# Layer 0's softmax sums in four 32-column tiles, with the reciprocals spread by DMA

## The chip, the core and the metric

The kernel runs on one core of a Trainium2 chip. The metric is the time of one execution in microseconds (us). PE is the matmul engine (TensorE), ACT is ScalarE, DVE is VectorE, POOL is GpSimd; SP is the engine that issues most DMAs. [...] the runs shown agree within 0.1%.

## What is computed

Two layers follow each other on four images of 32x32 tokens with 768 channels. Each adds to its input an attention of 12 heads of 64 channels, with a bias by row and by column of the image. The change touches the end of layer 0's attention:

```python
attn = (attn.reshape(b * NH, h, w, h, w) + rel_bias_h[:, :, :, :, None] + rel_bias_w[:, :, :, None, :]).reshape(b * NH, hw, hw)
attn = jax.nn.softmax(attn, axis=-1)
out = jnp.einsum('bqk,bkd->bqd', attn, v)
```

The kernel takes exponentials of the scores without their maximum, multiplies them by the values, and divides by the sum of the exponentials afterwards. So for every query of every head it needs one sum over 1024 keys and one reciprocal of it, and 64 channels of the result are multiplied by that reciprocal.

## The kernel before

The work is ordered in stages: (image 0, layer 0), (image 1, layer 0), (image 0, layer 1), (image 1, layer 1), and then the same for images 2 and 3. A stage has six pairs of heads; a pair fills the 128 partitions, one head in each half. `attend` (L720) handles one pair. It takes the queries in two halves c of QC = 512 columns, and the keys of each in two groups of four tiles of 128. For a group PE computes the scores s (L820) and adds the bias (L822), ACT takes the exponentials e (L827), and after some other work PE multiplies them by the values into av (L844). In layer 0 DVE adds the eight exponential tiles of a half into `acc` (L836, L838), one column block for each head.

The order on PE, ACT, DVE and POOL is the order in which the program is written; only SP's queue is ordered by the framework. `attend` gives way four times in each half, and a table of events runs pieces of other work at these steps: the next pair's projections and its bias (`positions`, PE line L613, tile rel), the projection of the stage before, weights that are mixed in the first stage, normalisation.

What is left to do for a half when its av is finished is held in the list `rest` and done one part at a time by `more()`, which is called four times in a half: after the scores and after the products with the values of each key group. For layer 0 the parts are `sums`, `result` and `finish`:

- `copy` (L742), at once: ACT copies av from PSUM into `weighed`, which has one buffer.
- `sums` (L788 to L793), at the first call of the next half: PE multiplies a matrix of ones with `acc` into the PSUM tile z, for each head 64 columns of ones, so that all 64 partitions of the head hold the same sums (two matmuls of 512 columns; L789). ACT copies z to t, and takes Ln and Exp of it to get a first reciprocal `inv`.
- `result` (L800, L801, L807), at the second call: DVE corrects the reciprocal by one Newton step in two instructions, and multiplies `weighed` by it.
- `finish` (L812), at the third: ACT adds the bias of the values and writes the result over the pair's q.

Layer 1 gets its sums in another way, from a column of ones among the values; its first DMAs (L748, L749) carry one row of `weighed` to DRAM and spread it over 64 partitions into t, issued by POOL. It shares `weighed`, t and inv with layer 0. `put_q`, `put_k` and `centre`, `back` (PE lines L556, L591; tiles ln_c, ln_t) make layer 1's queries and keys; DVE's taps (L542, L544) are its convolutions. The last pair of a layer-0 stage that is followed by layer 1 has these beside its own attention.

Weight loads for the projections go through SP (L250, L253, L254, L263) into two buffers: the load for the use after the next is issued when a use is done.

Of the kernel before, what the change touches and what calls it, by code (L numbers as in the profile page):

```python
# [9 lines left out]
F32 = mybir.dt.float32  # L10
F32R = mybir.dt.float32r
I32 = mybir.dt.int32
AF = mybir.ActivationFunctionType
ALU = mybir.AluOpType
# [3 lines left out]
P = 128  # L18
B = 4
S = 32  # L20
T = S * S
C = 768
NC = C // P
D = 64
HALF = T // 2
QC = 512
# [7 lines left out]
LN = 75  # L34
# [3 lines left out]
IDENT, GROUP, CENTRE, HEADS, ONES, WHOLE = 0, P, 2 * P, 3 * P, 3 * P + 2, 3 * P + 2 + D  # L38
# [7 lines left out]
def two_layers(ctx: ExitStack, tc: tile.TileContext, keep, x_in, wqkv, wproj, rels, windows, vrow, small, const, onehot, picks, out):  # L46
# [19 lines left out]
    nc = tc.nc  # L66
    pool = lambda name, bufs, **kw: ctx.enter_context(tc.tile_pool(name=name, bufs=bufs, **kw))
    fixed = pool("fixed", 1)
    dram = pool("dram", 1, space=bass.MemoryType.DRAM)
    xnp = pool("xnp", 1)  # L70
    wp = pool("wp", 2)
    work = pool("work", 2)
    one = pool("one", 1)
# [41 lines left out]
    def other_work(places):  # L115
        turn[:] = places
        place_b.n = place_c.n = 0
# [7 lines left out]
    def small_bank(name):  # L125
        return ps_small.tile([P, 512], F32, tag="small", name=name)
# [14 lines left out]
    cst = fixed.tile([P, NCONST], F32, tag="cst", name="cst")  # L141
# [5 lines left out]
    def col(c, lo=0, hi=P):  # L147
        return sm[lo:hi, c : c + 1]
# [222 lines left out]
    seen = fixed.tile([P, 2 * len(items) * (T // QC)], F32, tag="seen", name="seen")  # L371
    tiny = fixed.tile([P, 1], F32, tag="tiny", name="tiny")
# [342 lines left out]
            return pieces  # L715


    rest, found = [], ()

    def attend(pair, os):  # L720


        q, k, bias = pair.q, pair.k, pair.bias


        by_ones = [pair.layer and (pair.i < len(items) - 1 or c < T // QC - 1) for c in range(T // QC)]
        os.append(q)
        nonlocal found
        heads = [slice(j * D, (j + 1) * D) for j in range(2)]

        def more():
            nonlocal found
            if rest:
                found = rest.pop(0)(*found)

        for c in range(T // QC):
            cols = slice(c * QC, (c + 1) * QC)

            def copy(av, ones=by_ones[c]):

                weighed = one.tile([P, QC], F32, tag="weighed", name="weighed")
                nc.scalar.copy(weighed, av)  # L742
                if not ones:
                    return weighed, acc
                t = work.tile([P, QC], F32, tag="t", name="t", bufs=1)

                z = dram.tile([2, QC], F32, tag="z", name="z", bufs=2)
                nc.gpsimd.dma_start(z, weighed[D - 1 :: D, :])  # L748
                nc.gpsimd.dma_start(t, z.unsqueeze(1).to_broadcast([2, D, QC]))  # L749
                return weighed, t  # L750

            def restore(weighed):

                ps = small_bank("whole")
                halves(ps, cst[:, WHOLE : WHOLE + P], weighed)
                nc.scalar.copy(weighed, ps)

            def restore_last(weighed):

                ps = small_bank("last")  # L760
                odd = cst[:, WHOLE + 1 : WHOLE + P : 2]
                for h in range(2):
                    nc.tensor.matmul(
                        ps[h * D : (h + 1) * D, : QC // 2], odd, weighed[:, h * (QC // 2) : (h + 1) * (QC // 2)],
                        start=True, stop=True,
                    )
                last = one.tile([P, QC // 2], F32, tag="last", name="last")
                nc.scalar.copy(last, ps[:, : QC // 2])  # L768
                for h in range(2):
                    rows = last[h * D + D // 2 - 1 : (h + 1) * D : D // 2, :]  # L770
                    nc.gpsimd.dma_start(weighed[D - 1 :: D, h * (QC // 2) : (h + 1) * (QC // 2)], rows)  # L771

            def landed(*found):

                return found

            def sums(weighed, of, c=c, ones=by_ones[c]):

                at = 2 * (pair.i * (T // QC) + c)
                inv = work.tile([P, QC], F32, tag="inv", name="inv", bufs=1)  # L780
                if ones:
                    t = of
                    restore_last(weighed)
                    nc.scalar.activation(inv, t, AF.Copy, accum_out=seen[:, at : at + 1])
                else:
                    z = small_bank("z")
                    t = work.tile([P, QC], F32, tag="t", name="t", bufs=1)
                    for j, rows in enumerate(heads):  # L788
                        nc.tensor.matmul(z[rows, :], cst[:, ONES : ONES + D], of[:, j, :], start=True, stop=True)  # L789
                    nc.scalar.activation(t, z, AF.Copy, accum_out=seen[:, at : at + 1])  # L790

                nc.scalar.activation(inv, t, AF.Ln, bias=tiny)
                nc.scalar.activation(inv, inv, AF.Exp, scale=-1.0, accum_out=seen[:, at + 1 : at + 2])  # L793
                if pair.layer and not ones:
                    restore(weighed)
                return weighed, t, inv

            def result(weighed, t, inv, cols=cols):

                nc.vector.scalar_tensor_tensor(t, t, -1.0, inv, ALU.mult, ALU.mult)  # L800
                nc.vector.scalar_tensor_tensor(inv, t, 2.0, inv, ALU.add, ALU.mult)  # L801

                if pair.layer:
                    nc.vector.tensor_tensor(inv, weighed, inv, ALU.mult)
                    nc.vector.scalar_tensor_tensor(q[:, cols], inv, col(LN + 4), q[:, cols], ALU.mult, ALU.add)
                else:
                    nc.vector.tensor_tensor(inv, weighed, inv, ALU.mult)  # L807
                return (inv,)

            def finish(inv, cols=cols):  # L810

                nc.scalar.activation(q[:, cols], inv, AF.Identity, bias=col(pair.column(2)))  # L812

            for g in range(0, NKT, 4):
                es = []
                for kt, place in zip(range(g, g + 4), (None, place_b, place_c, None)):
                    keys = slice(kt * P, (kt + 1) * P)
                    ps = place.pair("s") if place else ps_a.tile([P, 2, 512], F32, tag="a", name="s")
                    for j, rows in enumerate(heads):
                        nc.tensor.matmul(ps[:, j, :], k[rows, keys], q[rows, cols], start=True, stop=False)  # L820
                    for j, rows in enumerate(heads):
                        nc.tensor.matmul(  # L822
                            ps[:, j, :], ones[rows, kt % 2 * P : (kt % 2 + 1) * P], bias[c][rows, kt // 2, :],
                            start=False, stop=True,
                        )
                    e = work.tile([P, 2, QC], F32, tag="e", name="e", bufs=4)
                    nc.scalar.activation(e, ps, AF.Exp)  # L827
                    es.append(e)
                other_work(behind_scores)
                more()  # L830
                if g == 0:
                    av = ps_av.tile([P, QC], F32, tag="av", name="av")
                if not by_ones[c]:
                    if g == 0:
                        acc = work.tile([P, 2, QC], F32, tag="acc", name="acc", bufs=1)
                        nc.vector.tensor_tensor(acc, es[0], es[1], ALU.add)  # L836
                    for e in es[2 * (g == 0) :]:
                        nc.vector.tensor_tensor(acc, acc, e, ALU.add)  # L838
                yield
                yield  # L840
                for t, e in enumerate(es):
                    kt = g + t
                    for j in range(2):
                        nc.tensor.matmul(  # L844
                            av[j * D : (j + 1) * D, :], pair.vt[:, kt, j * D : (j + 1) * D], e[:, j, :],
                            start=(kt == 0), stop=(kt == NKT - 1),
                        )
                other_work(behind_av)
                more()
                if g + 4 == NKT:  # L850

                    n_parts = 2 if short(pair.i) and (pair.hp, c) in ((NC - 2, 1), (NC - 1, 0)) else 1
                    rest.extend((landed,) * n_parts + (sums, result) if pair.layer else (sums, result, finish))
                    found = copy(av)
                yield
                yield
# [161 lines left out]
    for k, stage in enumerate(stages):  # L1018
        call, sums, products = project(stage, oss[k])
# [27 lines left out]
    for _ in range(2):  # L1047
        found = rest.pop(0)(*found)
    next(products)
    for part in rest:  # L1050
        found = part(*found)
# [314 lines left out]
```

## Time and profile before

| | |
|---|---|
| median of 3 runs | 3814.33 us (3814.24 to 3817.77) |
| the profiled execution, whole | 3816.61 us |
| its span in the trace | 3814.6 us |
| granted PE clock | 0.997 of full |
| z, t (ACT copy), Ln, Exp: each | 4 matmul records, 0.60, 0.72, 0.63 us |
| DVE's two steps of the correction, each | 0.68, 0.69 us |
| DMA to landing: mid<-x (256 KB, SP) | 3.1 us |
| DMA to landing: t<-z (256 KB, POOL) | 8.0 us |
| DMA to landing: z<-weighed (4 KB, POOL) | 1.6 us |

In lines of groups the first columns are the line, engine, operation, output and inputs; for PE the tile shape follows (rows*columns of the array), then the operands' shape and the count; behind the first bar stand the total busy time in us and the mean of one in ns; behind the second the idle time of the engine just before. In the list of waits the numbers are the total in us, the times and the longest. In the timeline the first two numbers are the start and the busy time in us, and brackets at the end hold the idle time before and what ended it. [...] records overlap; the distance between starts is the time that the work takes.

### The profile page before, as it was taken

The numbers are of one execution on the slowest core, as the hardware profiler recorded it, in microseconds if no ns is written. First come the engines' busy times: TensorE is split into PE (matmuls) and PEld (weight loads), VectorE is DVE, ScalarE is ACT, GpSimd is POOL, SyncE is SP. The second block draws the span as 40 slices with busy tenths as digits, with TensorE's granted clock in tenths as the row PEclk, the third lists the DMA queues.
The fourth block names the chain that finished last, engine by engine and source line by source line (L and its number), as shares of the span: only waits on it lengthen the run. The fifth ranks groups of instructions, "written<-read, shape, count | busy, mean of one in ns | idle before, by whom it ended". The sixth has DMA issues, their size and how long they took to land. (4 is left out here: it accounts for less than half of the span.)

```text
span 3814.6 us, 76313 instructions
## 1 busy us (share of the span) xinstructions
PE 3749.5 (98%) x32990; PEld 1656.7 (43%) x32990; DVE 2467.1 (65%) x3068; ACT 1786.5 (47%) x2573; POOL 529.1 (14%) x964
## 2 busy tenths in 40 slices
PE   8999999999999999999999999999999999999998
PEld 4535535533344443444535445355343444434442
DVE  2566554559678877688454554445686888867874
ACT  2455434545355553455534544254442555525562
POOL 0111100111111211111200010001111112111120
PEclk9999999999999999999999999999999999999999
DMA  4344443331431223311333132523114212142123
GB/s 152 102 122 116 134 144 90 101 81 40 119 102 48 57 59 95 123 48 48 82 111 121 53 78 63 171 61 78 46 46 131 87 50 66 47 122 65 48 58 100
DMA packets 214024, 330.44 MB, mean 87 GB/s; under 512 B 50390, under 2 KB 103698, under 8 KB 213680
## 3 DMA queue, kind: packets, MB, share of 16 engines
q1 hardware_dynamic: 122912, 211.86, 17.9%
q0 software_dynamic: 90768, 113.61, 12.6%
q8 instruction: 263, 4.31, 0.5%
q14 instruction: 81, 0.66, 0.1%
HBM read 184.23 MB, written 40.10 MB: 59 GB/s over the span
## 5 line engine op out<-in xcount | busy, mean ns | idle before, releaser
L827 ACT ACTIVATE e<-s 128x1024 f32<-128x1024 f32 x768 | 775.6, 1024 | 423.7 <-PE s L822 393.6
L131 PE MATMUL qkv<-xn,wqkv_t 128*64 128x512 f32 x3648 | 816.0, 596 | 7.0 <-DVE gmean L334 2.6
L820 PE MATMUL s<-q,k 64*128 64x512 f32 x3072 | 808.7, 603 | 6.6 <-ACT e L827 3.1
L544 DVE SCALAR_TENSOR_TENSOR shared<-shared,sm 128x1056 f32<-128x1056 f32 x576 | 757.9, 1316 | 15.7
L822 PE MATMUL s<-bias,ones 64*128 64x512 f32 x1536 | 611.7, 790 | 1.1 <-DMA bias<-whole 1.0
L844 PE MATMUL av<-e,vt 128*64 128x512 f32 x2624 | 596.2, 596 | 0.0
L131 PEld LDWEIGHTS qkv<-xn,wqkv_t 128*64 128x64 f32 x3648 | 256.5, 137 | 484.0 <-issue 466.1
L640 POOL DMA_DIRECT2D bias<-high x384 | 205.6, 556 | 1794.6 <-ACT high L629 1559.7
L838 DVE TENSOR_TENSOR acc<-acc,e 128x1024 f32<-128x1024 f32 x294 | 360.0, 1225 | 114.0 <-ACT e L827 87.4
L820 PEld LDWEIGHTS s<-q,k 64*128 64x128 f32 x3072 | 279.5, 186 | 264.4 <-issue 213.3
L527 ACT ACTIVATE shared<-qkv,sm 128x512 f32<-128x512 f32 (+1 forms) x288 | 129.3, 502 | 469.7 <-PE qkv L131 469.7
L844 PEld LDWEIGHTS av<-e,vt 128*64 128x64 f32 x2624 | 185.4, 137 | 350.9 <-issue 316.8
L822 PEld LDWEIGHTS s<-bias,ones 64*128 64x128 f32 x1536 | 148.6, 187 | 185.4 <-issue 184.1
L640 POOL DMA_DIRECT2D bias<-whole x384 | 207.2, 571 | 53.2 <-DVE whole L630 46.3
L836 DVE TENSOR_TENSOR acc<-e 128x1024 f32<-128x1024 f32 x49 | 60.0, 1225 | 215.4 <-ACT e L827 206.8
L742 ACT COPY weighed<-av 128x512 f32<-128x512 f32 x96 | 56.3, 587 | 279.0 <-PE av L844 270.1
L559 DVE TENSOR_REDUCE mean<-ln_c 128x8 f32<-128x512 f32 x144 | 98.6, 685 | 106.0 <-PE ln_c L556 106.0
L771 POOL DMA_DIRECT2D weighed<-last x94 | 50.7, 541 | 679.6 <-ACT last L768 638.6
L613 PEld LDWEIGHTS rel<-q,rel 64*32 64x32 f32 x6144 | 112.1, 106 | 68.6 <-issue 63.8
L613 PE MATMUL rel<-q_t,rel 64*32 64x32 f32 x6144 | 123.6, 195 | 1.8 <-issue 1.8
L613 PE MATMUL rel<-q,rel 64*32 64x32 f32 x6144 | 122.7, 195 | 1.9 <-issue 1.9
L412 DVE TENSOR_TENSOR shared<-shared,m3m 128x512 f32<-128x512 f32 x66 | 45.3, 687 | 119.9 <-PE m3m L131 119.8
(162 smaller groups left out, 4439.0 us busy)
## 6 DMA issues: line engine op xcount, KB each, us to landing
bias<-high POOLq DMA_DIRECT2D x384, 128.0 KB, 2.9
bias<-whole POOLq DMA_DIRECT2D x384, 128.0 KB, 3.0
wqkv_t<-in_wqkv SPq DMA_DIRECT2D x78, 384.0 KB, 3.2
wqkv_t<-mixed SPq DMA_DIRECT2D x66, 384.0 KB, 3.1
wproj_t<-mixed SPq DMA_DIRECT2D x48, 384.0 KB, 3.3
wqkv_t<-in_wqkv SPq DMA_DIRECT2D x66, 192.0 KB, 2.5
xn<-in_x SPq DMA_DIRECT2D x24, 512.0 KB, 7.7
x<-in_x SPq DMA_DIRECT2D x48, 256.0 KB, 3.2
```

Of the source, the lines that this page charges most:

```text
L131: nc.tensor.matmul(ps[lo : lo + D], a[:, lo : lo + D], b, start=start, stop=stop, **kw)
L527: nc.scalar.activation(self.pad[s][:, rows, there : there + src.shape[2]], src, AF.Identity, bias=col(self.column(s)))
L544: nc.vector.scalar_tensor_tensor(y, window, tap, y, ALU.mult, ALU.add)
L559: nc.vector.tensor_reduce(of, heads, AX.X, ALU.add)
L613: nc.tensor.matmul(ps[lo : lo + S, k * S : (k + 1) * S].rearrange("p (b c) -> p b c", b=2), rel[rows, 2 * self.layer + i, first : first + ...
L640: nc.gpsimd.dma_start(sets, some.unsqueeze(1).to_broadcast([D // 2, 2, QC]))
L820: nc.tensor.matmul(ps[:, j, :], k[rows, keys], q[rows, cols], start=True, stop=False)
L822: nc.tensor.matmul(ps[:, j, :], ones[rows, kt % 2 * P : (kt % 2 + 1) * P], bias[c][rows, kt // 2, :], start=False, stop=True,)
L827: nc.scalar.activation(e, ps, AF.Exp)
L836: nc.vector.tensor_tensor(acc, es[0], es[1], ALU.add)
L838: nc.vector.tensor_tensor(acc, acc, e, ALU.add)
L844: nc.tensor.matmul(av[j * D : (j + 1) * D, :], pair.vt[:, kt, j * D : (j + 1) * D], e[:, j, :], start=(kt == 0), stop=(kt == NKT - 1),)
```

## The change

For all layer-0 halves but the last of each stage, `sums` multiplies `acc` by 32 columns of ones instead of 64, and takes each head's 512 columns in two parts of 256: four matmuls, each into its own 32 partitions of z. ACT's copy, Ln and Exp and DVE's correction then work on 256 columns. `spread` writes one row of each 32 (4 rows of 256) to DRAM from SP's queue; `call`, one step later, reads it back over 64 partitions for each head into t. `spread_finish` puts the multiplication into a list `unfinished`; the next call of `more()`, the first of the half after, takes it from there, and the one after that writes q. So the product comes two calls after its reciprocals are called, and q is written three calls later than before. The last half of a stage keeps the old way, and before it reuses t what is unfinished is done at once. `weighed` gets two buffers, in both layers.

```diff
         def more():
             nonlocal found
+            for piece in [unfinished.pop() for _ in range(len(unfinished))]:
+                piece()
+            if rest and getattr(rest[0], "reuses", False):
+                while unfinished:
+                    unfinished.pop()()
             if rest:
                 found = rest.pop(0)(*found)
...
-                weighed = one.tile([P, QC], F32, tag="weighed", name="weighed")
+                weighed = one.tile([P, QC], F32, tag="weighed", name="weighed", bufs=2)
...
+                if not pair.layer and not last(c):
+
+                    z = small_bank("z")
+                    for j in range(2):
+                        for h in range(2):
+                            g, n = 2 * j + h, QC // 2
+                            nc.tensor.matmul(
+                                z[g * S : (g + 1) * S, :n], cst[:, ONES : ONES + S], of[:, j, h * n : (h + 1) * n],
+                                start=True, stop=True,
+                            )
+                    both = work.tile([P, 2, QC // 2], F32, tag="inv", name="z_inv", bufs=1)
+                    t, inv = both[:, 0], both[:, 1]
+                    nc.scalar.activation(t, z[:, : QC // 2], AF.Copy, accum_out=seen[:, at : at + 1])
+                    nc.scalar.activation(inv, t, AF.Ln, bias=tiny)
+                    nc.scalar.activation(inv, inv, AF.Exp, scale=-1.0, accum_out=seen[:, at + 1 : at + 2])
+                    return weighed, t, inv
...
+            def last(c):
+
+                return (pair.hp, c) == (NC - 1, T // QC - 1)
+
+            sums.reuses = last(c)
...
+            def spread(weighed, t, inv):
+
+                newton(t, inv)
+                z = dram.tile([2, QC], F32, tag="z_inv", name="z_inv", bufs=2)
+                nc.sync.dma_start(z.rearrange("j (h x) -> (j h) x", h=2), inv[S - 1 :: S, :])
+                return weighed, z
+
+            def call(weighed, z):
+
+                t = work.tile([P, QC], F32, tag="t", name="t", bufs=1)
+                nc.sync.dma_start(t, z.unsqueeze(1).to_broadcast([2, D, QC]))
+                return weighed, t
+
+            def spread_finish(weighed, t, cols=cols):
+
+                def multiply():
+                    nc.vector.tensor_tensor(t, weighed, t, ALU.mult)
+                    unfinished.append(lambda: finish(t, cols))
+
+                unfinished.append(multiply)
+                return ()
...
-                    rest.extend((landed,) * n_parts + (sums, result) if pair.layer else (sums, result, finish))
+                    rest.extend((landed,) * n_parts + (sums, result) if pair.layer else (sums, result, finish) if last(c) else (sums, spread, call, spread_finish))
```

`newton` holds DVE's two instructions of L800 and L801.

More of the change, by code (lines that the diff above doesn't have):

```diff
@@ L715, in plan @@
             return pieces
-    rest, found = [], ()
+    rest, found, unfinished = [], (), []
     def attend(pair, os):
@@ L796, in sums, with newton, result @@
                 return weighed, t, inv
-            def result(weighed, t, inv, cols=cols):
+            def last(c):
+                return (pair.hp, c) == (NC - 1, T // QC - 1)
+            sums.reuses = last(c)
+            def newton(t, inv):
                 nc.vector.scalar_tensor_tensor(t, t, -1.0, inv, ALU.mult, ALU.mult)
                 nc.vector.scalar_tensor_tensor(inv, t, 2.0, inv, ALU.add, ALU.mult)
[L803 to L808, printed above, removed]
+            def result(weighed, t, inv, cols=cols):
+                newton(t, inv)
+                nc.vector.tensor_tensor(inv, weighed, inv, ALU.mult)
+                if not pair.layer:
+                    return (inv,)
+                nc.vector.scalar_tensor_tensor(q[:, cols], inv, col(LN + 4), q[:, cols], ALU.mult, ALU.add)
+                return ()
+            def spread(weighed, t, inv):
+                newton(t, inv)
+                z = dram.tile([2, QC], F32, tag="z_inv", name="z_inv", bufs=2)
[10 more added lines that the diff above has]
+                unfinished.append(multiply)
+                return ()
             def finish(inv, cols=cols):
                 nc.scalar.activation(q[:, cols], inv, AF.Identity, bias=col(pair.column(2)))
+                return ()
             for g in range(0, NKT, 4):
```

## The prediction

> **What bounds the kernel now.** I read the page's busy shares first, then the waits of the matmul engine, then the groups by line for the rows that the change touches, then the timeline around them.
>
> ```profile
> PE 3749.5 (98%) x32990; PEld 1656.7 (43%) x32990; DVE 2467.1 (65%) x3068; ACT 1786.5 (47%) x2573; POOL 529.1 (14%) x964
> ```
> ```profile
> PE p1p L131 <- DVE os_sums L923: 7.4, 8, 1.6
> PE ln_t L591 <- DVE shared L560: 6.1, 7, 1.9
> ...
> PE s L820 <- ACT e L827: 3.1, 3, 1.4
> ```
> ```profile
> L789 PE MATMUL z<-acc,cst 128*64 128x512 f32 x196 | 52.8, 617 | 0.0
> L807 DVE TENSOR_TENSOR inv<-weighed,inv 128x512 f32<-128x512 f32 x48 | 33.2, 692 | 1.6
> L812 ACT ACTIVATE q<-inv,sm 128x512 f32<-128x512 f32 x48 | 34.2, 712 | 0.0
> L763 PE MATMUL last<-weighed,cst 128*64 128x256 f32 x188 | 28.9, 381 | 0.0
> ```
>
> PE is busy 98% of the span, and the largest waits of single causes on it are a few us over the whole run. So only two things can move the time: fewer cycles that PE streams, and one of the few places where another engine holds it. VectorE and ScalarE have a third to a half of the span free; their savings count only at such places. The sums of exponentials (z) are 196 matmul records for 49 pieces of work, four each: two heads in two column halves, and each float32 product in two passes. They never wait (idle 0.0).
>
> Now the same block in the timeline, three times:
>
> ```profile
> 201.56 1.08 PE L789 MATMUL z<-acc,cst 128*64 128x512 f32 x4
> 202.47 2.74 PE L131 MATMUL m4m<-xn,wqkv_t 128*64 128x512 f32 x12
> ```
> ```profile
> 237.93 1.08 PE L789 MATMUL z<-acc,cst 128*64 128x512 f32 x4
> 238.94 0.21 PE L613 MATMUL rel<-q,rel 64*32 64x32 f32 x1
> ```
> ```profile
> 1050.03 0.60 PE L763 MATMUL last<-weighed,cst 128*64 128x256 f32 x4
> 1050.46 1.89 PE L131 MATMUL qkv<-xn,wqkv_t 128*64 128x512 f32 x8
> ```
>
> From start to start, z costs 0.91 us when the next work has the same tile shape (128*64), and 1.01 us when the shape changes behind it (rel, 64*32): the change of shape costs 0.10. The row "last" has half the columns (256) in the same two column halves and costs 0.43. So time follows the columns streamed, 0.21 us per pass of 256 columns, with two column halves side by side.
>
> [...] No row of before shows four 128-row tiles of 32 columns; the nearest is rel, whose four tiles (two row halves, four column groups) start every 7 to 10 ns (888.59, 888.59, 888.60, 888.61) and last 190 ns, so four column groups do run at once there, but each half of the rows feeds only two of them. [...] the trace's 4 KB z<-weighed lands in 1.6.
>
> **The change part by part.** Layer 0 has 48 pieces (24 pairs of heads, two halves of the queries); the last of each of its four stages keeps the old way, so 44 change.
>
> *Matmuls.* Per piece 2 matmuls of 64x512 become 4 of 32x256, all four at once if the tiles are independent: a pass falls from 0.43 to 0.21, two passes save 0.43 us. From this go: (a) the stagger of four starts instead of two, 14 ns per pass by the 7 ns between two starts, 0.03; (b) a change of shape behind z where there was none. By the order of instructions the 44 are followed by rel 21 times and ln_c twice (a change of shape before and after, so nothing new: the nearest price is again 0.10), and 21 times by 128*64 work (m4m 18, av 2, v 1). There I add 0.10 for the change and 0.05 for the first pass behind a change (by the starts of its single records z's own first pass, behind s, takes 0.48, the second 0.43). Sum: 23 x 0.40 + 21 x (0.40 - 0.15) = 9.2 + 5.3 = 14.5 us. Bounds: if the four share two streams, z stays 0.9 and the extra changes cost 21 x 0.15 + 44 x 0.03 = 4.5 us; if the shape changes cost nothing, 44 x 0.43 = 19.
>
> *ScalarE and VectorE arithmetic.* Copy, Ln and Exp go from 512 to 256 columns: about 0.21 us less each (the copies of this kernel take 0.586 at 512 and 0.372 at 256), 44 x 0.6 = 28 us of ScalarE. The two VectorE steps of the correction lose about 0.27 each (0.69 at 512 columns, 0.55 at 384, so some 0.41 at 256), 44 x 0.55 = 24 us. Both beside PE's work, worth nothing in general.
>
> *The place where they are worth something.* The last layer-0 pair of stages two and six prepares layer 1, and VectorE there is busy without a gap from 877 to 920 us (46.1 of 50 us from 880 to 930, and 46.4 from 2780 to 2830), and PE waits for it:
>
> ```profile
> 910.70 0.66 PE L591 MATMUL ln_t<-cst,shared 128*128 128x128 f32 x4
> 913.24 0.63 PE L591 MATMUL ln_t<-cst,shared 128*128 128x128 f32 x4 [1.88 <-DVE shared L560]
> ```
>
> In this stretch the correction is 0.55 shorter and its product (0.69) goes to the next pair, where VectorE has a gap of 2.4 us; the product of the piece before comes in at 876, in a gap of 0.7. That is 1.2 us earlier at 913, less some 0.2 to 0.4 of PE's gain from z there that VectorE doesn't pass on: 1 us a time, 2 us in all. Between 0 and 3.
>
> *Transfers on SP.* Each piece adds two issues to SP's queue: the reciprocals to DRAM (waits for VectorE's correction) and from there spread to 128 partitions (waits for the first to land and for the last reader of t). Behind them in the queue stand the weight loads. By the order of instructions the next old issue comes in nearly all pieces 6.6 us or more after the correction ended in the trace of before (186.3 behind 179.7), in two pieces 3.5; the pair takes some 0.4 to issue and 1.6 to 2 to land, so SP is free again after about 2.5. The exceptions wait for nothing urgent: two pieces have stores of mixed weights next, which VectorE makes later anyway, and one has loads for a projection some 50 us away. Even if a weight load slips, it has room: the load of 186.3 is used at 202.5. Cost taken: 0; up to 2.
>
> *The product and its wait.* VectorE's product now waits for the spread reciprocals, and behind it in VectorE's queue stand the additions into acc, whose end z and PE wait for; ScalarE's write of q waits for the product, and exponentials stand behind that. From the end of the correction to the first addition it stands before, the trace of before has 22 to 24 us in most pieces (179.7 to 202.8) and 10.8 in six (247.2 to 258.0). Write and spread need about 0.4 + 2 + 0.4 + 3 = 6 us by the hardware rows of similar size (mid<-x 256 KB 3.1), 10.5 if the spread takes the 8.0 of GpSimd's t<-z. Both fit. Cost taken: 0; up to 1 at the six.
>
> *The second buffer for weighed.* Needed, as the product comes after the next copy. In layer 1 it also takes away ScalarE's wait for the product of the piece before (4.5 us at 2 places, one more 4.5 that is named for L582). PE there waits for keys that VectorE still has to make, so 0; up to 2 gained.
>
> *Sum.* 14.5 + 2 = 16.5, less 0.5 as the middle of the small costs: 16 us. The traced execution took 3816.6, its span 3814.6 and 2.0 around it; 16 us less is 3800.6 for that execution. Against the median of the runs, 3814.3, it is 3798.
>
> **The rivals.**
> *A, the forecast*: four groups at once and no new wait, 3798, its own range 3792 to 3804 (the price of the shape changes, 0 to 0.25 each). Chance 0.72.
> *B, the tiles don't do what they are meant to*: 128 rows by four groups of 32 columns stream at half rate. For it: no row of before has them. Against: rel. Then 4.5 lost, 2 gained at VectorE's stretch, 0.5 lost: 3817, no change. Chance 0.11.
> *C, the wait moves to the product (the slower one)*: VectorE stands at the product because the spread lands late behind bulk transfers, and PE waits at z. The point: over about 23 us from the correction in most pieces, plus 4 us for which the buffers of e let VectorE lag. At 28 us each piece costs PE 1 us, 44 in all: 3814 + 44 - 16 = 3842. For it: DMA engines are 40% busy in the first 880 us, and loads of a whole input (six of 512 KB, 7.7 us each) share the queue. Against: four times the cover. Chance 0.08.
> *D, more than the sum*: the freed VectorE and ScalarE time also shortens the short waits elsewhere (s on exponentials 3.1 us, ln_t 6.1, p1p 7.4 in the list above) and the second buffer pays in layer 1: 24 us, 3790. Chance 0.09.
>
> **How the numbers follow.** A measurement of this kernel can tell about 0.2%, 7.6 us, from no change. A and D lie beyond it (0.81), and B's upper part, tiles partly at once, adds 0.02: faster 0.83. The rest of B is the same, 0.09, and C slower, 0.08. For eight in ten I keep A with D's near part below, and of B the part where half of the gain stays: 3789 to 3811.
>
> **What would show it.** Right: z as records of 32 columns by 256, with about 0.66 us to the next start before m4m (0.91 now) and 0.61 before rel (1.01 now); PE's busy time down by about 14; the wait of 1.88 at ln_t near 0.9 or less; no wait of VectorE at the product, none of PE on z. Wrong: z still near 0.9 (B); idle time before the product put down to the DMA of t, and PE waits at z or s that before lacks (C); or waits of PE for weights behind the new issues on SP.

## The result, and the profile after

The changed kernel takes 3808.61 us as median of 20 runs (3801.84 to 3814.79); the kernel before, run beside it, 3815.49 us (20 runs, 3813.2 to 3817.77). The ratio is 0.9981, with a 95% interval of 0.9975 to 0.9987: faster by 6.9 us, where 16 were forecast. The direction was right, the size was not: the time lies within the forecast's range only at its upper end. The profiled execution took 3810.16 us with a span of 3808.1, 6.5 less than the span before.

First the busy times on the page of the changed kernel, and then its waits on the matmul engine (total in us, times, longest):

```profile
PE 3734.4 (98%) x33166; PEld 1655.9 (43%) x33166; DVE 2440.7 (64%) x3068; ACT 1750.4 (46%) x2573; POOL 526.2 (14%) x964
```
```profile
PE p1p L131 <- DVE os_sums L976: 7.4, 8, 1.6
PE s L875 <- DMA bias<-whole: 7.0, 4, 2.9
PE ln_t L591 <- DVE shared L560: 4.1, 7, 0.8
PE s L873 <- ACT e L880: 3.9, 4, 1.4
```

PE's busy time fell by 15.1 us, VectorE's by 26.4, ScalarE's by 36.1. But the span fell by only 6.5, so the gap between PE's busy time and the span grew by 8.6 us. One entry is new in the list: the bias product of the scores waits for a load of the bias. Before, the same wait came to 1.0 us, once. The wait at ln_t went from 6.1 to 4.1.

The groups by line show what became of the pieces' own instructions:

```profile
L856 DVE TENSOR_TENSOR t<-weighed,t 128x512 f32<-128x512 f32 x44 | 30.1, 684 | 36.2 <-DMA t<-z_inv 36.2
L792 PE MATMUL z<-acc,cst 128*32 128x256 f32 x352 | 28.1, 391 | 0.0
L799 ACT ACTIVATE z_inv<-z_inv,tiny 128x256 f32<-128x256 f32 x44 | 22.4, 508 | 1.4
L829 DVE SCALAR_TENSOR_TENSOR z_inv<-z_inv 128x256 f32<-128x256 f32 x44 | 18.7, 425 | 1.5
L800 ACT ACTIVATE z_inv<-z_inv 128x256 f32<-128x256 f32 x44 | 18.3, 417 | 1.4
L828 DVE SCALAR_TENSOR_TENSOR z_inv<-z_inv 128x256 f32<-128x256 f32 x44 | 18.1, 412 | 0.0
```

The last part of the first line is the one that the forecast had excluded: VectorE sits idle 36.2 us before the product, for the spread reciprocals. All of it falls on six of the 44 pieces, 4.08 to 7.42 us each, and these are the six with the short cover that the prediction put at 10.8 us (10.8 to 12.2 in the trace of before).

The same places in the timeline of the changed kernel as were shown of before, z in front of m4m, z in front of rel, and ln_t:

```profile
201.31 0.64 PE L792 MATMUL z<-acc,cst 128*32 128x256 f32 x8
201.88 2.79 PE L131 MATMUL m4m<-xn,wqkv_t 128*64 128x512 f32 x12
...
237.40 0.64 PE L792 MATMUL z<-acc,cst 128*32 128x256 f32 x8
237.97 0.21 PE L613 MATMUL rel<-q,rel 64*32 64x32 f32 x1
...
910.80 0.66 PE L591 MATMUL ln_t<-cst,shared 128*128 128x128 f32 x4
912.30 0.63 PE L591 MATMUL ln_t<-cst,shared 128*128 128x128 f32 x4 [0.85 <-DVE shared L560]
```

From start to start z now costs 0.57 us in both cases (0.91 and 1.01 before), and the stall at ln_t is 0.85 (1.88 before).

Last, the timeline around the first of the six pieces. "SPq L850" is the spread's issue, "POOL L640" are the bias loads, brackets hold the idle time and what ended it:

```profile
247.12 2.08 POOL L640 DMA_DIRECT2D bias<-whole  x4 [1.56 <-DVE whole L630]
...
247.87 0.52 SPq L850 DMA_DIRECT2D t<-z_inv  x1
...
249.17 2.11 POOL L640 DMA_DIRECT2D bias<-high  x4
...
251.22 1.10 POOL L640 DMA_DIRECT2D bias<-whole  x2
...
254.71 0.50 PE L875 MATMUL s<-bias,ones 64*128 64x512 f32 x2 [2.35 <-DMA bias<-whole]
...
254.85 0.53 POOL L640 DMA_DIRECT2D bias<-whole  x1 [2.54 <-DMA bias<-whole]
...
259.14 0.69 DVE L856 TENSOR_TENSOR t<-weighed,t 128x512 f32<-128x512 f32 x1 [4.08 <-DMA t<-z_inv]
...
260.07 0.64 PE L792 MATMUL z<-acc,cst 128*32 128x256 f32 x8
```

Two things are late here. The spread is called at 247.87, and its product starts only at 259.14, 11.3 us later. And the bias loads, which POOL issues in the same microseconds, are late too: PE stands 2.35 us for one of them, and POOL itself 2.54 before it can issue its next one.

### The profile page after: what moved, and what is told of

The parts are those of the page before. It is cut to its first block, busy times and chain, and to the rows that moved or that the text cites. A ratio compares the mean times of both kernels' runs of the same rounds, so it can differ in the third digit from the quotient of the medians.

```text
span 3808.1 us, 76869 instructions
## 1 busy us (share of the span) xinstructions
PE 3734.4 (98%) x33166; PEld 1655.9 (43%) x33166; DVE 2440.7 (64%) x3068; ACT 1750.4 (46%) x2573; POOL 526.2 (14%) x964
## 2 busy tenths in 40 slices
DMA packets 220097, 342.17 MB, mean 90 GB/s; under 512 B 50654, under 2 KB 104138, under 8 KB 219752
## 3 DMA queue, kind: packets, MB, share of 16 engines
q1 hardware_dynamic: 128984, 223.58, 18.7%
q0 software_dynamic: 90768, 113.61, 12.5%
## 4 chain that ended last, share of the span: by engine, by line
PE 45%; DVE 5%; ACT 1%; DMA 1%; issue 1%; POOL 0%; DVEq 0%; SPq 0%; ACTq 0%; POOLq 0%
PE qkv L131 9%; PE s L873 8%; PE av L897 8%; PE m4m L131 3%; PE m1m L131 2%; PE m3m L131 2%; PE s L875 2%; PE p3p L131 2%; PE p4p L131 2%; PE p1p L131 2%; PE rel L613 1%; PE m L131 1%; DVE shared L544 1%; PE ln_c L556 1%; DVE acc L891 1%
## 5 line engine op out<-in xcount | busy, mean ns | idle before, releaser
L640 POOL DMA_DIRECT2D bias<-high x384 | 202.7, 548 | 1798.7 <-ACT high L629 1561.1
L640 POOL DMA_DIRECT2D bias<-whole x384 | 207.2, 571 | 48.2 <-DVE whole L630 31.1
L131 PE MATMUL m3m<-xn,wqkv_t 128*64 128x512 f32 x528 | 120.9, 592 | 2.3 <-DVE shared L412 2.3
```

The costliest lines, as they stand in the source:

```text
L131: nc.tensor.matmul(ps[lo : lo + D], a[:, lo : lo + D], b, start=start, stop=stop, **kw)
L640: nc.gpsimd.dma_start(sets, some.unsqueeze(1).to_broadcast([D // 2, 2, QC]))
```

## The experiments

Two theories were set against each other for the missing 9 us, and the expectations name them: W, the late product (VectorE stands at it, and its later work stands behind: the additions into acc, for which z waits, and the mixing of weights, for which PE's m3m waits), and H, the two new transfers holding up the bias loads, so that PE waits for these. That they would do so by holding DMA engines, as the expectations put H, is not shown: the trace doesn't name the engine of a packet. Every kernel was compared with the kernel before on the same chip; the table gives the medians and what was gained.

| kernel | median us (range) | before | ratio, 95% | gain us |
|---|---|---|---|---|
| the change | 3808.61 (3801.84–3814.79) | 3815.49 | 0.9981 [0.9975, 0.9987] | 6.9 |
| e1 no transfers | 3798.57 (3796.01–3799.95) | 3814.85 | 0.9956 [0.9942, 0.9970] | 16.3 |
| e2 product one call later | 3804.89 (3800.96–3811.28) | 3814.85 | 0.9972 [0.9961, 0.9983] | 10.0 |
| e3 before + transfers | 3844.50 (3842.72–3849.99) | 3814.85 | 1.0080 [1.0067, 1.0094] | −29.7 |
| e4 spread as two DMAs | 3795.88 (3793.08–3801.57) | 3814.85 | 0.9951 [0.9937, 0.9965] | 19.0 |
| e5 e4, product late by four copies | 3822.74 (3815.01–3825.95) | 3814.89 | 1.0017 [1.0010, 1.0025] | −7.9 |
| e6 before + second buffer | 3812.74 (3809.84–3814.57) | 3814.89 | 0.9992 [0.9984, 1.0001] | 2.2 |
| e7 before + two-DMA transfers | 3823.86 (3819.89–3825.97) | 3814.89 | 1.0022 [1.0013, 1.0032] | −9.0 |
| e8 e4, layer 1's spread also in two | 3793.81 (3792.17–3794.97) | 3814.89 | 0.9942 [0.9929, 0.9956] | 21.1 |
| e9 e4, product late by three copies | 3800.75 (3799.25–3803.95) | 3815.29 | 0.9963 [0.9950, 0.9977] | 14.5 |
| e10 e4 + an unread DMA | 3796.06 (3793.45–3798.36) | 3815.29 | 0.9950 [0.9936, 0.9964] | 19.2 |
| e11 before + the four matmuls | 3801.18 (3800.79–3803.06) | 3815.29 | 0.9964 [0.9951, 0.9978] | 14.1 |
| e12 e4 + two unread DMAs | 3795.44 (3795.20–3798.36) | 3814.18 | 0.9953 [0.9939, 0.9967] | 18.7 |

**e1, the change without its two transfers.** The multiplication takes the 256 columns of reciprocals that lie in its own partitions, twice; half of the results are then divided by other sums, and VectorE has one instruction more per piece.

```diff
-                nc.sync.dma_start(z.rearrange("j (h x) -> (j h) x", h=2), inv[S - 1 :: S, :])
...
-                nc.sync.dma_start(t, z.unsqueeze(1).to_broadcast([2, D, QC]))
...
-                    nc.vector.tensor_tensor(t, weighed, t, ALU.mult)
+                    for h in range(2):
+                        part = slice(h * (QC // 2), (h + 1) * (QC // 2))
+                        nc.vector.tensor_tensor(t[:, part], weighed[:, part], inv, ALU.mult)
```

> The changed kernel without the two transfers of each piece: the product uses the 256 reciprocals that lie in the same partition (two VectorE products of 256 columns at the same place), so the division is left out of its proper rows. Theory W (VectorE stands at the product because the spread lands 11 us after its issue) and theory H (the packets of the spread hold DMA engines, the loads of bias land late and PE waits at the scores) both expect the whole loss gone: z gains 23 x 0.44 + 21 x 0.34 = 17 us in the trace, and 2 us at ln_t, so 3796 against 3815.5. Rival Z (the matmul block gains less in the whole than its records say) expects it to stay near 3808.

Measured: 16.3 us gained, and no wait of PE for a bias load is left in its list. So the transfers, with the waits that they bring, take what is missing, and nothing else in the change does.

**e2, the product one call of `more()` later.**

```diff
-                unfinished.append(multiply)
+                unfinished.append(lambda: unfinished.append(multiply))
```

> The product one call of more() later, after the additions of the next half's first group, transfers as they are. W: VectorE's waits of 4 to 7 us at six products go, nearly all of the loss goes, about 3797. H: the spread still holds the DMA engines, PE still waits some 7 us for bias<-whole, 3805 to 3809.

Measured: 10.0 us gained. VectorE's waits at the six products are gone, but two of about 9 us come up at other pieces, products at 467.6 and 2352.1 us, whose spread is called only at 457.2 and 2342.0 (the first of them at 447.7 in the change). PE still waits 4.5 us for a bias load at one place. The interval overlaps that of the change, so at most a part comes back; the edit brings waits of its own and can't weigh W against H.

**e3, the transfers alone in the kernel before.** The same write and the same spread for every piece, into a tile that nobody reads; z and the correction stay as before, and the product stays in its place but goes into t, since the write still reads inv.

```diff
+                z = dram.tile([2, QC], F32, tag="z_inv", name="z_inv", bufs=2)
+                nc.sync.dma_start(z.rearrange("j (h x) -> (j h) x", h=2), inv[S - 1 :: S, : QC // 2])
...
+                    spare = work.tile([P, QC], F32, tag="spare", name="spare", bufs=1)
+                    nc.sync.dma_start(spare, z.unsqueeze(1).to_broadcast([2, D, QC]))
```

> The kernel before (64 columns of ones, product at its old place) with the same two transfers for each of the 44 pieces, into a tile that nobody reads. H: PE waits for bias<-whole as in the changed kernel, 6 to 12 us slower than before, 3822 to 3827. W: nobody waits for the spread, 3815 to 3817.

Measured: 29.7 us lost, more than was expected, with nobody waiting for the data. Its list of waits on PE begins with

```profile
PE s L830 <- DMA bias<-whole: 17.4, 6, 3.6
```

at the same six pieces at which the product waits in the change. In this kernel H is shown without W.

**e4, the spread as two DMAs, one for each head.** Same bytes, same source, same place in SP's queue.

```diff
-                nc.sync.dma_start(t, z.unsqueeze(1).to_broadcast([2, D, QC]))
+                for j, rows in enumerate(heads):
+                    nc.sync.dma_start(t[rows, :], z[j : j + 1, :].to_broadcast([D, QC]))
```

> The changed kernel with the spread as two DMAs, one for each head (source 64 times the same row of 512), instead of one whose source goes over 2 rows 64 times each. If the slow landing comes from how the one DMA is dealt out over the DMA engines (about 1.5 of its packets in flight), it lands in 3 to 5 us, W and H both expect about 3797. If it comes from all packets reading the same 4 KB of DRAM, it still takes 9 to 11 us and the time stays near 3808.

Measured: 19.0 us gained; this version beats both kernels, and its interval stands clear of the change's. Its timeline at the same piece:

```profile
246.41 2.08 POOL L640 DMA_DIRECT2D bias<-whole  x4 [1.56 <-DVE whole L630]
...
248.13 1.11 SPq L851 DMA_DIRECT2D t<-z_inv  x2
...
248.46 2.11 POOL L640 DMA_DIRECT2D bias<-high  x4
...
250.51 1.61 POOL L640 DMA_DIRECT2D bias<-whole  x3
...
252.33 0.53 POOL L640 DMA_DIRECT2D bias<-whole  x1 [0.21 <-issue]
...
254.27 0.68 DVE L857 TENSOR_TENSOR t<-weighed,t 128x512 f32<-128x512 f32 x1
...
255.06 0.64 PE L792 MATMUL z<-acc,cst 128*32 128x256 f32 x8
```

The product follows the call by 6.1 us and has no wait, and POOL's last bias loads go out at once. Over the run VectorE waits 1.3 us for t and PE 0.8 us for a bias load. z stands at 255.06, 5.0 us earlier than in the change; 0.7 of these it already had at the head of this stretch (POOL's first line).

How the one DMA differs from the two can be read from the packets. The DMA queues on the pages (packets, MB, share) of the change and of e4:

```profile
q1 hardware_dynamic: 128984, 223.58, 18.7%
```
```profile
q1 hardware_dynamic: 130304, 223.58, 19.0%
```

At equal bytes e4 has 1320 packets more, all of them under 512 B (51974 against 50654 on the pages): 30 for each of the 44 pieces. The packets of 2 KB themselves, counted in the trace:

```
one DMA:  128 packets from 249.75 to 258.66 (8.9 us), median 98 ns
two DMAs: 128 packets from 249.51 to 252.38 (2.9 us)
```

The times of the one DMA's packets add up to 13.2 us within these 8.9, so on average 1.5 of them are under way at once. Over how many of the DMA engines either is dealt out is not shown.

**e5 and e9, W alone.** e4 with three (e9) or four (e5) copies of the 4 KB from DRAM to DRAM ahead of the spread, one after the other, at the six pieces; they make the product late with hardly any traffic.

```diff
+                if pair.i in (2, 4, 8, 26, 28, 32) and cols.start == 0:
+                    for k in range(4):
+                        hop = dram.tile([2, QC], F32, tag=f"hop{k}", name="hop", bufs=1)
+                        nc.sync.dma_start(hop, z)
+                        z = hop
```

> The kernel of e4 (spread dealt out well) with four copies of 4 KB from DRAM to DRAM put before the spread at the six pieces whose product waited, some 2 us each, so that t lands as late there as in the changed kernel but holds no DMA engine. W: VectorE waits 4 to 8 us six times again and the loss comes back with it, 3804 to 3810. H: the late product alone costs little, 3796 to 3801.

> As e5 with three copies in place of four, so that VectorE's wait at the six products comes near the 6.0 us each of the changed kernel (8.8 in e5) with no DMA engine held. W (the wait is most of the changed kernel's loss of 12.7 us against e4): 3806 to 3810. H (the held engines are most of it): 3797 to 3802.

Measured: four copies give waits of 53.0 us on VectorE, 8.8 a piece, and cost 27 us against e4, more than either theory expected; with three it is 39.3 us, 6.5 a piece, close to the 6.0 of the change, and the cost is about 4.5 us against e4, with intervals that overlap (3800.75 lies in the range that H expected). The waits on PE, of e5 and then of e9:

```profile
PE m3m L131 <- DVE shared L412: 17.5, 6, 4.9
```
```profile
PE m3m L131 <- DVE shared L412: 4.4, 5, 2.4
```

No PE wait above 0.8 us for the bias is there in e9. So at the lateness of the change W by itself costs some 4.5 of the 12 us that lie between the change and e4, not clear of nothing, and 2.3 us more per piece would have made it dear.

**e6, the second buffer alone**, the kernel before with `bufs=2` for `weighed` and nothing else.

> The kernel before with the second buffer of weighed and nothing else. All theories of the transfers: no change, 3813 to 3816. A rival for part of the gain (layer 1 gets rid of ScalarE's waits, 9 us in three places): up to 4 us faster, 3811.

Measured: 2.2 us gained, with an interval that includes no change.

**e7, e3 with its spread as two DMAs** (the edit of e4 made in e3).

> The traffic of e3 into the unread tile, but dealt out as two DMAs for each piece, the same bytes. H in the form that it is the dealing and not the bytes: PE's waits for bias<-whole (17.4 us in e3) go and the time is 3814 to 3818. If the bytes themselves did it: still above 3835.

Measured: 9.0 us lost instead of 29.7, between the two expectations, and the wait for the bias loads is

```profile
PE s L831 <- DMA bias<-whole: 4.1, 4, 1.9
```

So 21 of e3's 30 us come from the spread being one DMA and not two. The other 9 are what the same transfers, with the spread in two DMAs, and the moved product cost in the kernel before; they weren't taken apart. In e4 this price isn't seen. One difference is the time: at the first of the six pieces of e7 the spread goes out at 249.00, 0.2 us ahead of POOL's four `whole` loads, and in e4 1.7 us behind them.

**e8, e4 with layer 1's GpSimd spread (L754, `t<-z`) in two DMAs as well.**

```diff
-                nc.gpsimd.dma_start(t, z.unsqueeze(1).to_broadcast([2, D, QC]))
+                for j, rows in enumerate(heads):
+                    nc.gpsimd.dma_start(t[rows, :], z[j : j + 1, :].to_broadcast([D, QC]))
```

> The kernel of e4 with layer 1's spread of its sums (GpSimd's t<-z, 47 times, 7.9 us to landing) also in two DMAs, one for each head. If dealing is what makes that one slow too, it lands in 3 to 4 us, ScalarE's wait for it at the end of layer 1 (2.6 us in the trace of before) goes and the time falls by 1 to 4 us, to 3792 to 3795. If GpSimd's queue deals out otherwise: as e4, 3796, or 1 us slower for 47 further issues.

Measured: the best median, 21.1 us gained, though not told apart from e4. ScalarE's wait for this DMA (2.3 us in e4) is gone. The landing of that DMA, in the trace's list of issues (KB, us to landing), of e4 and of e8:

```profile
t<-z POOLq DMA_DIRECT2D x47, 256.0 KB, 7.9
```
```profile
t<-z POOLq DMA_DIRECT2D x94, 128.0 KB, 2.8
```

The same two-row source, the same cure, on another queue.

**e10 and e12, further spreads from two rows, with nobody waiting.** e4 with a third DMA per piece (e10), or two more (e12), whose source again has two rows, of 256 columns each, and whose data nobody reads. e12 moves as many bytes in DMAs from two rows as the change does; to make room for its second tile, a constant matrix that isn't used is left out of SBUF.

```diff
+                spare = one.tile([P, QC // 2], F32, tag="last", name="spare")
+                nc.sync.dma_start(spare, z[:, : QC // 2].unsqueeze(1).to_broadcast([2, D, QC // 2]))
```

> The kernel of e4, and behind its two DMAs a third for each piece, dealt out as the changed kernel's one (2 rows of 256, 64 times each) into a tile that layer 0 doesn't read. Nothing waits for it, the product has its reciprocals early. H: PE waits for bias<-whole again, 4 to 10 us in the trace, and the time is 3801 to 3808. W: 3795 to 3798.

> As e10 with the full bytes of the changed kernel's spread: two such DMAs for each piece, 128 packets of 1 KB each, into two tiles that layer 0 doesn't read (constants that these layers don't use are left out of SBUF to make room). H: PE waits for bias<-whole, 4 to 10 us in the trace, 3801 to 3808. If it stays at 3794 to 3798, the packets of the badly dealt DMA alone don't delay the bias at the changed kernel's own timing, and H rests on e3's timing.

Measured: 19.2 and 18.7 us gained, so no loss against e4, against what H expected. e10 has 136024 packets on SP's queue, 5720 more than e4, 44 times the 128 of data and 2 more. PE's wait for a bias load is 1.7 us at one place in both, against 0.8 in e4. Such transfers alone therefore cost nothing that shows. What differs from the change is when they go out, and that this decides is argued, not shown: here they go behind the two fast ones, and at the first of the six pieces of e12 POOL begins its four `whole` loads at 244.15, 1.6 us ahead of the call of t at 245.71; in the change it begins them at 247.12, 0.8 us ahead of the call. Later bias loads have a slow tail in e12 as well (11 to 14 packets started per us from 253 to 256), with PE not waiting for them.

**e11, the four matmuls alone.** The kernel before with z as four tiles of 32 columns, and ScalarE's first copy reading the 256 columns twice so that all that follows keeps 512. The sums aren't brought to their rows, so the division is by other sums.

```diff
+                        for g in range(4):
+                            nc.tensor.matmul(
+                                z[g * S : (g + 1) * S, :n], cst[:, ONES : ONES + S], of[:, g // 2, g % 2 * n : (g % 2 + 1) * n],
+                                start=True, stop=True,
+                            )
```

> The kernel before with the four 32-column matmuls alone; ScalarE copies the 256 columns twice to fill t, and everything behind it works on 512 columns as before, so the sums are not brought to their rows (left out) and no transfer is added. If the matmuls carry the gain as their records say (0.91 and 1.01 us to 0.57): 17 us faster, 3796 to 3799. If a good part of e4's gain is VectorE's and ScalarE's shorter work: only 8 to 13 us faster, 3802 to 3807.

Measured: 14.1 us gained, between the two expectations.

**PE's waits and its clock, in all traces.** The trace also records the clock that is granted to PE, as a share of the full one. Here are the microseconds around the first bias wait of the change, and the same stretches of e4 (stretch and length, PE's busy time and matmuls, granted clock, DMA share, GB/s):

```profile
245.00:255.00 10.00, 7.65 (x38) 1.00 0.86 221
255.00:259.00 4.00, 4.00 (x16) 0.58 0.78 233
```
```profile
245.00:255.00 10.00, 10.00 (x52) 1.00 1.02 225
255.00:259.00 4.00, 4.00 (x26) 1.00 0.86 247
```

The 0.58 is 3.4 us at half the clock, from 255.6 on, right behind the wait. The 14 traces hold 44 such stretches while PE still has work to do, each 3.4 or 6.8 us long, and in the 3.4 us before each of them PE was idle for 1.8 to 3.4 us. Not every wait of 2 us is followed by one: that of 2.34 us at m3m, 397.3 us into the change, isn't. So in these runs a long wait of PE can be paid twice, once as idle time and once as work at half the clock. The table splits the span of each profiled execution accordingly: PE's idle time (span less busy time), half of PE's busy time in the stretches of half clock, and what is left.

| kernel | span us | PE idle | lost at half clock | PE's work at full clock |
|---|---|---|---|---|
| before | 3814.6 | 65.1 | 8.0 | 3741.5 |
| e3 | 3842.7 | 83.9 | 16.5 | 3742.3 |
| e7 | 3818.1 | 70.9 | 5.1 | 3742.1 |
| e11 | 3798.9 | 66.9 | 5.0 | 3727.0 |
| the change | 3808.1 | 73.7 | 6.7 | 3727.7 |
| e4 | 3794.1 | 65.7 | 1.6 | 3726.8 |
| e9 | 3797.9 | 67.4 | 3.2 | 3727.3 |
| e5 | 3821.6 | 81.1 | 13.3 | 3727.2 |

The last column falls into two groups, the old z and the new one, some 15 us apart and each within 1 us, which supports the halving. What else sets these kernels apart is idle time of PE and half clock: between e9 and e5, 23.7 us apart, the one grows by 13.7 and the other by 10.1, and between before and e3, 28.1 apart, by 18.8 and 8.5.

## Why the prediction was right on the matmuls and wrong on the transfers

**Matmuls: right.** "Sum: 23 x 0.40 + 21 x (0.40 - 0.15) … = 14.5 us". e11 measures 14.1, and PE's work at full clock fell by 13.8 in the change and by 14.5 in e11. The four groups run at once (in the block at 201.31 their records start 7 ns apart and take 0.40 us each, and the second pass starts 0.24 us after the first), so rival B falls. The starts in the records would give somewhat more (23 x 0.44 + 21 x 0.34 = 17 us), as the step to m4m took 0.57 and not the 0.66 of the forecast; e11's interval, 8.4 to 18.7 us, holds both, and the table is nearer to the forecast.

**ScalarE and VectorE arithmetic, and the place at ln_t: right.** 412 and 425 ns for the correction against 0.41 forecast; the wait at ln_t fell by 2.0 us, as forecast. e4 gains 4.9 us more than e11, while the sum had 2 for this. In their profiled executions, 4.8 apart, the idle time makes about 1 of it and the half clock 3.4; what the second buffer adds is open (e6: 2.2, not settled).

**Transfers on SP: right in what they were priced for.** PE's one wait for weights from SP is 0.9 us in the changed kernel (0.5 before).

**The product and its wait: wrong; here the forecast failed.** The step was: "Write and spread need about 0.4 + 2 + 0.4 + 3 = 6 us …, 10.5 if the spread takes the 8.0 of GpSimd's t<-z. Both fit. Cost taken: 0; up to 1 at the six." Four things were wrong in it.

First, the landing. From the call to the product the six pieces took 10.5 to 11.5 us, not 3.4 and not 8.4. The price of 3.1 was taken from mid<-x, a DMA of the same size; the row t<-z has the same source form, two rows repeated, and its 8.0 was the right one to start from. That the form of the one DMA is the cause, and not its bytes, is shown by e4 (8.9 us for the packets of one DMA, 2.9 for those of two) and e8 (7.9 and 2.8 to landing).

Second, the point of comparison. 10.5 (10.8 by its own terms) against a cover of 10.8 was called a fit. It left nothing. The write before the spread took 2.0 to 3.1 us at the six, as priced, so the product came 12.6 to 14.6 us after the end of its correction. The six pieces named were the six that waited. By e9 this alone costs some 4.5 us.

Third, the prediction asked who waits for the new transfers, but not whom they hold up. In the packets of the change, between 254 and 256 us only 9 to 11 bias packets start per us, of some 110 ns each, where there were over 100 per us from 250 to 254. With the 10 to 14 of the spread that makes about 20 to 25 per us, so by count times length 2 to 3 of the two kinds together are under way at once. Meanwhile some 205 packets per us of stores of mixed weights start, of some 65 ns each, so not every transfer is slow. That these last bias packets stand behind those of the spread is the author's estimate; the trace doesn't show what a packet waits for. PE waits 7.0 us for these loads in the change, 0.8 in e4, and e3 shows such a loss where no product waits at all.

Fourth, the cost of a wait was taken as its length. The change and e4 are 14.0 us apart in their profiled executions: 8.0 of idle time, 5.1 of half clock and about 1 of work. The waits for the bias make 6.2 of the idle time, and two stretches of half clock (255.6 and 2143.2 us) stand behind them, 3.4 us more. The late products show as one wait of PE, 2.34 us at m3m, behind the product at 394.5. So in this pair of executions H is the larger part and W the smaller. That is one execution of each; by the medians the split is open, since e9 and the change stand on overlapping intervals, and e10 and e12 show that spreads from two rows don't do it by themselves.

The change's 20 runs lie 13 us apart (0.3%), those of the kernel before 4.6 (0.1%). The granted clock goes with it: 0.999 in the two shortest of the 20 and 0.997 in the five longest, and 0.002 of the span is 7.6 us. Why the waits differ from run to run wasn't tested.

**The rivals.** C had VectorE's wait at the product right, and the wrong measure: it asked for 23 us in every piece and so for 44 hits, where six with a short cover sufficed. It also had PE waiting at z, where PE in fact waits for the bias and once at m3m. D's total lies near what was there to be had, e8's 3793.8 against 3790, but by luck: the wait at p1p stayed at 7.4 us, that of s for exponentials went from 3.1 to 3.9, and e8's gain includes an edit that D doesn't have. With the spread in two DMAs the change gives 3795.9 (e4), 2 us below the forecast's 3798.

## What to carry to other kernels

Price a new DMA by the row with the same form of source, not by the same number of bytes (here 8.0 us against 3.1, and the spread's packets took 8.9), and where a broadcast has two outer rows, as here, try a DMA for each (2.9 us here). Then ask two questions of a transfer that is added: what is the shortest cover among all its uses (not the usual one), and which loads of other queues are in flight when it goes out. A wait that this brings to PE may cost more than its length (here 6.2 us of idle time and 3.4 of half clock behind it).

## What was not expected of the hardware

- One 256 KB spread from two rows takes 8.9 us, the same bytes in two DMAs 2.9 (the change and e4, first of the six pieces, from the first packet to the last). Layer 1's on GpSimd's queue went from 7.9 to 2.8 (e4 and e8), and there GpSimd's queue has 20304 packets fewer for it (70464 against 90768).
- A wait of VectorE isn't worth its length: 6.5 us at six places (e9) cost about 4.5 us in all, 8.8 us at the same places (e5) about 27; PE's idle time and its half clock grow with it by 13.7 and 10.1 us.
- All 44 stretches of half clock in the 14 traces, 3.4 or 6.8 us long, stand behind 3.4 us in which PE was idle for 1.8 us or more.
- The same bytes, in two DMAs and unread, still cost 9.0 us in the kernel before (e7) and nothing that shows in e4.
